# The last layer of a four-layer image network: the factors of its norms formed as pairs of matmuls, an output weight and a copy moved to VectorE, and the value projections placed later in the order

## The chip, the cores and the metric

The kernel runs on one core of one Trainium2 chip, as one program. The metric is the device time of one execution in microseconds (us); for the kernel before it is the median of three runs. Engines are named as in the profile: PE is TensorE's matmul side and PEld its weight loads, DVE is VectorE, ACT is ScalarE, POOL is GpSimd, SP is SyncE, which here only issues DMAs.

## The reference, cut to what matters

Eight images of 32 x 32 positions with 256 channels go through four layers, each `x = x + layer(groupnorm(x))`. The change lies in layer 3 alone:

```
qkv = silu(x @ w_qkv.T);  q, k, v = split(qkv)             # 8 heads of 32 channels
q = rope(rms_norm(q, w_qn));  k = rope(rms_norm(k, w_kn))  # norm over the 32 channels of a head
width, sharp = from silu(x @ w_wp.T + b_wp)                # the soft disc, per position and head
scores = q . k_win / sqrt(32)                              # 7 x 7 window around each position
scores -= (1 - sigmoid((width - rel_dist) * sharp)) * 10000
out = softmax(scores) @ v_win
out = rms_norm(out, w_on)                                  # norm over all 256 channels
y = silu((out + v) @ w_out.T)
```

The rope turns q and k by the index of the head, alike for both, so it cancels in the scores and the kernel leaves it out. Each head's norm gives one factor per position and head, and the output norm one factor per position, with a weight per channel.

## The kernel before, in words

Layer 3 (`layer3`, from line 1917 on) keeps channels on the 128 partitions: an image is two halves of 128 channels, that is four heads of 32 channels each. A **chunk** J is one image b and one half c (16 chunks, `b, c = divmod(J, 2)`). A chunk has eight **groups**; a group is a pair of 8 x 8 blocks of positions with their 14 x 14 windows (196 keys), for the four heads of the chunk. There are 128 groups, and the loop at the end of `layer3` does one per iteration n, in a software pipeline. Iteration n emits, in this order: `scores(n+3)` (L1632, 16 matmuls into four PSUM buffers), `exps(n)` (L1655, four ACT exponentials), filler units due at n, `logits(n+3)` (L1645, four DVE operations that free the four buffers), `turn(n-2, 0)` (L1673 transposes, L1678 DVE copy), `finish()`, `soft(n+5)` (L2043, four ACT tanhs), `divide(n)` (L1662 DVE reciprocal, L1663 POOL product), filler units due at n + 0.5, `turn(n-2, 1)`, `finish()`, `values(n-3)` (L1689, L1697), `masked(n+5)` (L2050, POOL).

Each engine works strictly in the order of emission (`manual_schedule`). The work of a chunk other than its groups is cut into **filler units** with a due iteration (`fill.add(at, unit)`). A unit issues its matmuls and ACT work at once and may return a function; that function (`rest`) is kept in `later` and called at the next `finish()`. The units the change touches or steps around:

- `project(J, s, h)`: four matmuls (L1982) give half h (512 positions) of q, k or v (s = 0, 1, 2) in a PSUM buffer; ACT forms a tanh of it (`half_silu`, L1967). The rest is DVE (L1992, L1994), and for q and k a square on POOL (L2002).
- `roots(J, b)`: the mean squares of q and k of chunk J, and of an image's attention output where one is due, each as rows of one PSUM buffer (L2062, L2069); then ACT takes the logarithm (L2077) and exponential (L2078) with a table load before (L2076) and one after (L2043). `fac[J]` holds the factors: rows 32(2s + h) for s and h.
- `head_scale(J, s, h)`: one product of 32 rows (L2084, two matmul instructions) spreads a factor over the 32 channels of each head into a buffer of the ring; the rest is a DVE multiplication of q or k with it (L2088).
- `tail_sq`, `tail_scale(J, b, c, h)`: the same for the output norm: square on POOL (L2112), product with `won`, whose row 8 holds the weight `w_on` (L2117), DVE multiplication (L2121), POOL addition of v (L2122).
- `in_strips(J)` lays v out in strips (POOL, L2098); `vturn(J, u)`, u = 0 to 4, transposes them (`value_unit`, L1706) and copies the PSUM buffer to v on ACT (L1711).
- `output(b, m, h)`: four matmuls (L2130), the same tanh (L1967), DVE product (L2137), POOL addition (L2139), DMA out. `discs(b, u)`: L2015 and a chain of small ACT and DVE operations.

PSUM has eight buffers of 512 columns, given out in turn (`ring`, tag "m"); whoever asks for the ninth waits until the first has been read. For a chunk due at n = 8J, the order before is: k and q projections at n-12 to n-10.5, `roots` at n-8, v projections at n-7.5 and n-7, `head_scale` k at n-6 and n-5.5 and q at n-5 and n-4.5, `in_strips` at n-6, `vturn` at n-2, -1.5, -1, -0.5 and +1.5. `tail_scale` of image b stands at 16b + 30, 30.5, 31 and 31.5; outputs at 16b + 33.5, 39, 39.5 and 41.5.

`First3.early` loads layer 3's constants while layer 2 runs; its third step, `weight`, writes the two halves of `w_on` into `won` after DVE has cleared that tile (L396, L400).

Of the kernel before, what the change touches and what calls it, by code (L numbers as in the profile page):

```python
# [12 lines left out]
ALU = mybir.AluOpType  # L13
# [19 lines left out]
def shape_constants():  # L33
    f = np.float32
    p = np.arange(P)
    k = {}

    k["k_id"] = np.stack(
        [np.eye(P), (p[:, None] // 8 == p[None] // 8) / 8.0], 1
    ).astype(f)  # L40


    same = (p[:, None] // 32 == p[None] // 32).astype(np.float64)
    k["k_hd"] = np.stack([np.eye(P) - same / 32, same / 32], 1).astype(f)
    half = (1.0 / (f(10000.0) ** np.linspace(0.0, 1.0, 16, dtype=f))).astype(f)
    angle = np.repeat(half, 2)[p % 32]
    ang = (np.arange(63, dtype=f)[None] * angle[:, None]).astype(f).astype(np.float64)
    sign = np.where(p % 2 == 0, -1.0, 1.0)[:, None]
    lam = np.log(1.0 - 2.0 ** (-2.0 - 5.0 * np.arange(HEADS) / HEADS))
    i = np.arange(SIDE)  # L50
    dist = np.abs(i[:, None] - i[None])
    s = 1.0 / np.sqrt(np.exp(lam[:, None, None] * dist).sum(-1))
    n = (s * 32.0 ** -0.5)[np.arange(8).reshape(2, 4)[:, p // 32]]
    k["k_rot"] = np.concatenate(
        [np.cos(ang), np.sin(ang) * sign, n.transpose(1, 0, 2).reshape(P, 64)], 1
    ).astype(f)
    delta = np.arange(-28, 32)
    row = np.abs(delta[None] - (p // 32)[:, None])
    col = np.abs((p % 32)[:, None] - i[None])
    m = np.exp(lam[:, None, None, None] * (row[:, :, None] + col[:, None, :])[None])  # L60
    m = m * s[:, None, None, :]
    k["k_ret"] = m.reshape(HEADS, P, 60 * 32).transpose(1, 0, 2).astype(f)


    head = (p[:, None] // 64 == p[None] // 64).astype(np.float64)
    k["k_l1"] = np.stack(
        [
            np.where(p[:, None] <= p[None], 0.0, MASK_OUT),
            p[:, None] // 4 == p[None] // 4,
            np.eye(P) - head / 64,  # L70
        ],
        1,
    ).astype(f)
    two = (p[:, None] // 64 == np.arange(2)[None]).astype(f)
    k["k_l1_sel"] = np.concatenate([two / 64, np.zeros((P, 30))], 1).astype(f)


    q, kn = np.arange(64), np.arange(NWIN)
    dr = kn[None] // 14 - (q // 8)[:, None] - 3
    dc = kn[None] % 14 - (q % 8)[:, None] - 3  # L80
    ok = (abs(dr) <= 3) & (abs(dc) <= 3)
    r = np.sqrt(dr.astype(f) ** 2 + dc.astype(f) ** 2)
    win = np.stack([np.where(ok, r, 0.0), np.where(ok, 0.0, -MASK_OUT)], 1)
    k["k_win3"] = np.tile(win, (2, 1, 1)).astype(f)
    one = np.zeros((P, 32), f)
    one[:, 8] = 1.0
    k["k_sel3"] = np.concatenate(
        [(p[:, None] // 32 == np.arange(32)[None]) / 32.0, one / 256.0], 1
    ).astype(f)
    k["k_spread"] = (p[:, None] % 32 == p[None] // 32).astype(f)  # L90
    return {n: np.ascontiguousarray(v) for n, v in k.items()}


# [12 lines left out]
def layouts(inputs):  # L106
    i = {n: np.asarray(v) for n, v in inputs.items()}
    x = i["x"]
    a = {}
    a["x"] = x.reshape(-1, C).T.reshape(2, P, -1).transpose(1, 0, 2)  # L110
    a["l0_w"] = np.stack([_wt(i["L0_conv_W" + n]) for n in "qkvo"], 1)
    a["l0_gb"] = np.stack([i["L0_conv_ln_g"], i["L0_conv_ln_b"]], 1)
    a["l1_up"] = _wt(i["L1_conv_W_up"])
    a["l1_down"] = _wt(i["L1_conv_W_down"])
    a["l1_if"] = _wt(np.concatenate([i["L1_conv_W_i"], i["L1_conv_W_f"]], 0))
    a["l1_par"] = np.concatenate(
        [i["L1_conv_conv_w"].reshape(4, P, 4).transpose(1, 0, 2)]
        + [_cols(i["L1_conv_" + n])[:, :, None] for n in ("conv_b", "skip")],
        2,
    )  # L120
    a["l1_blk"] = np.stack(
        [i["L1_conv_W" + n].reshape(4, P, 4).transpose(1, 0, 2) for n in "qkv"], 1
    )
    gb = np.stack([i["L1_conv_b_i"], i["L1_conv_b_f"]], 1)
    a["l1_gb"] = np.tile(gb, (P // 8, 1))
    nw = np.zeros((4, 32, 2, 64), np.float32)
    for q in range(2):
        nw[:, q, q] = i["L1_conv_norm_w"].reshape(4, 2, 64)[:, q]
    a["l1_nw"] = nw.reshape(P, P)
    a["l2_qkv"] = _wt(i["L2_conv_qkv_w"])  # L130
    a["l2_proj"] = _wt(i["L2_conv_proj_w"])
    qkv_b = i["L2_conv_qkv_b"]
    a["l2_par"] = np.concatenate([_cols(qkv_b), _cols(i["L2_conv_proj_b"])], 1)
    idx = near_index()
    rpb = i["L2_conv_rpb"].reshape(HEADS, -1)
    a["l2_rpb"] = np.where(idx[:, None] >= 0, rpb[:, idx].transpose(1, 0, 2), MASK_OUT).astype(
        rpb.dtype
    )
    a["l3_qkv"] = _wt(i["L3_conv_w_qkv"])
    a["l3_out"] = _wt(i["L3_conv_w_out"])  # L140
    a["l3_wp"] = _wt(i["L3_conv_w_wp"])
    a["l3_bwp"] = i["L3_conv_b_wp"]
    a["l3_qkn"] = np.concatenate(
        [np.tile(i["L3_conv_w_" + n], 4) for n in ("qn", "kn")]
    )
    a["l3_on"] = i["L3_conv_w_on"].reshape(2, P)
    a.update(shape_constants())
    return {n: np.ascontiguousarray(v) for n, v in a.items()}

# [202 lines left out]
class First3(First):  # L352
# [8 lines left out]
    def early(self):  # L361
# [25 lines left out]
        def factors():  # L387
            won, spread = self.won, self.spread
            nc.vector.tensor_scalar(self.bwp, self.bwp, 0.5, None, ALU.mult)
            nc.gpsimd.tensor_scalar(self.wo, self.wo, 0.5, None, ALU.mult)  # L390
            nc.vector.tensor_mul(won[:, 0], won[:, 0], won[:, 1])
            nc.vector.scalar_tensor_tensor(
                spread[:, 0], won[:, 0], -(32.0**-0.5) / MASK_SCALE, spread[:, 0],
                ALU.mult, ALU.mult,
            )
            nc.vector.memset(won, 0.0)  # L396

        def weight():
            for h in range(2):
                nc.sync.dma_start(  # L400
                    self.won[32 * h + 8 : 32 * h + 9], a["l3_on"].unsqueeze(0)
                )

        return [loads, factors, weight]

# [1195 lines left out]
class DiscStream(Stream):  # L1601
# [100 lines left out]
    def value_unit(self, strips, dst, u):  # L1702
        ps = self.ring("vt")
        for i in range(4):
# [3 lines left out]
                strips[:, col, 8 * r : 8 * r + 8].rearrange("p i j -> p (i j)"),  # L1708
                self.K.ident,
            )  # L1710
        self.nc.scalar.copy(  # L1711
            dst[: self.PART, 4 * u : 4 * u + 4, :],
            ps[: self.PART, :].rearrange("p (s c) -> p s c", c=P),
        )
# [202 lines left out]
def layer3(tc, K, src, dst, n_img, a, first):  # L1917
    nc = tc.nc
    pairs = disc_pairs()
    with tc.tile_pool(name="l3c", bufs=1, reuse_waits="tile") as cp, tc.tile_pool(  # L1920
# [14 lines left out]
        for i in range(3):  # L1935
            st.clear(i)
        K.ring = st.ring
        bwp, sel, spread, won = first.bwp, first.sel, first.spread, first.won
        wo, win, eps = first.wo, first.win, first.eps

        gn = first.gn
# [136 lines left out]
            nc.scalar.activation(r[:n], r[:n], AF.Exp, scale=-0.5)  # L2078
            fac[J] = r

        def head_scale(J, s, h):
            g = slice(32 * (2 * s + h), 32 * (2 * s + h) + 32)
            ps = st.ring("fac_ps")
            nc.tensor.matmul(ps, spread[g, s], fac[J][g], start=True, stop=True)  # L2084

            def rest():
                d = dest(J, s, h)
                nc.vector.tensor_mul(d, d, part(ps))  # L2088

            return rest  # L2090

# [11 lines left out]
        def vturn(J, u):  # L2103
            b, c = divmod(J, 2)
            if u == 0:
                st.v[b, c] = wk.tile([P, st.slots, P], F32, name="v", bufs=2)
            st.value_unit(strips, st.v[b, c], u)


        def tail_sq(b, c):  # L2110
            sqs["o", c] = wk.tile([P, L], F32, name="sq", bufs=4)
            nc.gpsimd.tensor_mul(sqs["o", c], st.o[b, c], st.o[b, c])  # L2112

        def tail_scale(J, b, c, h):
            g, hs = slice(32 * h, 32 * h + 32), slice(h * HALF, (h + 1) * HALF)
            ps = st.ring("fac_ps")
            nc.tensor.matmul(ps, won[g, c], fac[J][g], start=True, stop=True)  # L2117

            def rest():
                d = st.o[b, c][:, hs]  # L2120
                nc.vector.tensor_mul(d, d, ps)  # L2121
                nc.gpsimd.tensor_add(d, d, vT[b, c][:, hs])  # L2122

            return rest

# [26 lines left out]
        def plan_chunk(J):  # L2152
# [4 lines left out]
            for i in range(4):  # L2157
                s, h = 1 - i // 2, i % 2
                fill.add(n - 12 + i / 2, lambda s=s, h=h: project(J, s, h))
                fill.add(n - 6 + i / 2, lambda s=s, h=h: head_scale(J, s, h))  # L2160
            fill.add(n - 7.5, lambda: project(J, 2, 0))
            fill.add(n - 7, lambda: project(J, 2, 1))
            fill.add(n - 6, lambda: in_strips(J))

        def plan_image(b):
            n = 16 * b
# [12 lines left out]
                    fill.add(n - 10 + u / 2, lambda u=u: discs(b, u))  # L2179
            for c in range(2):  # L2180
                fill.add(n + 19 + c, lambda c=c: tail_sq(b, c))
                for h in range(2):
                    fill.add(
                        n + 30 + c + h / 2,
                        lambda c=c, h=h: tail_scale(2 * b + 4, b, c, h),
                    )
            for i in range(4):
                at = n + 32 + (1.5, 7, 7.5, 9.5)[i]
                fill.add(at - 3, lambda i=i: reload(b, i // 2, i % 2))
# [28 lines left out]
        def start():  # L2218
# [15 lines left out]
            masked(0)  # L2234
            roots(0, None)
            in_strips(0)
            for i in range(4):
                head_scale(0, 1 - i // 2, i % 2)()
            masked(1)
            for i in range(3, 9):  # L2240
                st.clear(i)
# [88 lines left out]
```

## Time and profile before

| | |
|---|---|
| runs before | 3370.86, 3371.83, 3379.88 us; median 3371.83 us |
| profiled execution | 3368.94 us, span 3367.2 us, mean granted clock 0.974 |
| PE busy | 3206.9 us, 95% of the span |
| ACT, DVE, POOL busy | 2247.9 us (67%), 2177.8 us (65%), 1490.2 us (44%) |
| DMA | 268.00 MB, mean 80 GB/s |

The page divides busy time by the whole span. In the list of windows each row gives a stretch, its length, and then for each engine the busy microseconds and the number of instructions, in the order PE, PEld, DVE, ACT, POOL, then the TensorE clock granted in that stretch (1.00 is full speed), the share of the DMA engines and GB/s. In the timeline and the chain of waits a row begins with its start and its length, then engine, line and tile; "xN" counts instructions that were merged, and square brackets give idle time before it and what ended it. In the list of groups a row gives line, engine, operation, result and operands, shape, count, then busy us and the mean ns of one, then the engine's idle time before them.

### The profile page before, as it was taken

Reading aid. Unit: us, or ns where it says so; the run is one execution under the profiler, and the core shown is the slowest. Engines: PE = TensorE matmul, PEld = TensorE weight load, DVE = VectorE, ACT = ScalarE, POOL = GpSimd, SP = SyncE. Lnnn points to the kernel's source line nnn. Section 1 sums busy time; section 2 is a strip of 40 time slices with the busy share of each in tenths; the row PEclk is TensorE's granted clock in tenths of the full one; section 3 lists DMA queues with packets and bytes.
Section 4 is the critical chain, followed back from the end, with each engine's and each line's share of the span. In section 5 each row is a group of like instructions: output and inputs, shape, how many; then the busy total and the mean of one; then the engine's idle time right before and its main releaser. Section 6 shows DMA issues by size and latency. Waiting matters only on the chain.

```text
span 3367.2 us, 77570 instructions
## 1 busy us (share of the span) xinstructions
PE 3206.9 (95%) x30760; PEld 1646.7 (49%) x30760; DVE 2177.8 (65%) x5559; ACT 2247.9 (67%) x5040; POOL 1490.2 (44%) x1069
## 2 busy tenths in 40 slices
PE   7999999999998998899999989999998999999997
PEld 3323323323222444666666755666664555555554
DVE  4776776776675666555555565666665667777775
ACT  3666666766666668554554446667776788889885
POOL 4233233223321011244444445343435667888777
PEclk9999999999999999999999999999999779999999
DMA  3000000000001666767777733111111001111001
GB/s 139 14 26 1 26 26 1 26 17 11 26 7 39 240 225 217 231 182 181 195 194 184 211 91 101 46 58 52 40 49 48 14 14 33 32 34 39 27 27 61
DMA packets 138911, 268.00 MB, mean 80 GB/s; under 512 B 9202, under 2 KB 77172, under 8 KB 130228
## 3 DMA queue, kind: packets, MB, share of 16 engines
q1 hardware_dynamic: 132164, 242.67, 23.7%
q10 hardware_dynamic: 6384, 20.37, 1.9%
q8 instruction: 243, 3.98, 0.5%
q14 instruction: 120, 0.98, 0.1%
HBM read 177.81 MB, written 85.20 MB: 78 GB/s over the span
## 4 chain that ended last, share of the span: by engine, by line
PE 71%; ACT 9%; DVE 6%; POOL 6%; issue 4%; DMA 3%; POOLq 0%; ACTq 0%; SPq 0%; DVEq 0%
PE s L675 7%; PE sm L693 6%; PE num L720 6%; PE qkv_ps L1763 5%; PE qkv_ps L1982 4%; PE dn_ps L1310 3%; PE up_ps L849 3%; PE qk_ps L550 3%; PE pt L1545 3%; PE pt L1673 2%; PE fac_ps L2084 2%; ACT e L2043 2%; PE o_ps L603 2%; PE pr_ps L1823 2%; PE o L1564 2%
## 5 line engine op out<-in xcount | busy, mean ns | idle before, releaser
L681 DVE TENSOR_TENSOR e<-s,ret 128x1024 f32<-128x1024 f32 x512 | 602.9, 1219 | 180.5 <-PE s L675 176.5
L685 ACT ACTIVATE ea<-e 128x1024 f32<-128x1024 f32 x512 | 535.1, 1054 | 268.1 <-DVE e L681 234.1
L675 PE MATMUL s<-qk,qk 32*128 32x512 f32 x2048 | 300.5, 640 | 2.4 <-POOL qk L567 1.7
L1531 POOL TENSOR_TENSOR e<-e,su 128x616 f32<-128x616 f32 (+2 forms) x128 | 157.3, 1229 | 270.3 <-DVE su L1530 239.2
L693 PE MATMUL sm<-ea,ones 128*32 128x512 f32 x2048 | 273.0, 604 | 2.0 <-DVE dn L701 2.0
L720 PE MATMUL num<-e,v 128*32 128x512 f32 x2048 | 266.6, 592 | 0.0
L1678 DVE COPY pts<-pt 112x512 f32<-112x512 f32 x256 | 175.9, 687 | 133.9 <-PE pt L1673 132.4
L2043 ACT ACTIVATE e<-win,disc 128x196 f32<-128x196 f32 x512 | 239.6, 544 | 0.2
L849 PE MATMUL up_ps<-x,wup 128*128 128x512 f32 x512 | 232.4, 606 | 4.8 <-ACT sz L889 2.3
L1663 POOL TENSOR_TENSOR e<-e,su 128x784 f32<-128x784 f32 x128 | 191.4, 1495 | 87.1 <-DVE su L1662 59.8
L1655 ACT ACTIVATE e<-e,mx 128x196 f32<-128x196 f32 x512 | 228.0, 453 | 0.0
L2050 POOL TENSOR_TENSOR e<-e,win 128x784 f32<-128x784 f32 x128 | 201.8, 1577 | 38.1 <-issue 31.5
L1526 ACT ACTIVATE e<-e,mx 128x154 f32<-128x154 f32 (+2 forms) x512 | 212.1, 425 | 0.0
L1053 POOL TENSOR_TENSOR d<-cmask,d 128x1024 f32<-128x1024 f32 x64 | 152.4, 2386 | 105.7 <-DMA d<-l1rows 105.7
L1982 PE MATMUL qkv_ps<-xq,w 128*128 128x512 f32 x384 | 192.0, 627 | 1.2 <-ACT fac L2077 1.2
L1062 ACT ACTIVATE d<-d,cols 128x128 f32<-128x128 f32 x512 | 164.0, 392 | 43.3 <-POOL d L1053 43.2
L1763 PE MATMUL qkv_ps<-x,w 128*128 128x512 f32 x384 | 181.3, 609 | 1.6 <-POOL x L236 1.6
L1673 PEld LDWEIGHTS pt<-idg,e 128*112 128x112 f32 x1024 | 120.5, 139 | 121.1 <-issue 89.9
L675 PEld LDWEIGHTS s<-qk,qk 32*128 32x128 f32 x2048 | 85.3, 183 | 184.2 <-issue 119.1
L1305 POOL TENSOR_TENSOR num<-num,sz 128x512 f32<-128x512 f32 x64 | 81.4, 1272 | 207.6 <-ACT vt L1106 109.6
L1673 PE MATMUL pt<-idg,e 128*112 128x128 f32 x1024 | 165.1, 287 | 8.4 <-DVE oT L1697 3.1
L876 DVE SCALAR_TENSOR_TENSOR cv<-xm,par,cv 128x512 f32<-128x512 f32 x192 | 140.7, 750 | 47.0 <-ACT cv L871 44.1
(243 smaller groups left out, 6711.7 us busy)
## 6 DMA issues: line engine op xcount, KB each, us to landing
d<-l1rows SPq DMA_DIRECT2D x64, 512.0 KB
x<-x SPq DMA_DIRECT2D x25, 1024.0 KB
x<-x SPq DMA_DIRECT2D x32, 512.0 KB
l1xm<-xm SPq DMA_DIRECT2D x16, 1024.0 KB
l1sz<-sz SPq DMA_DIRECT2D x16, 1024.0 KB
xv<-l1xm SPq DMA_DIRECT2D x32, 512.0 KB
l1xa<-xa SPq DMA_DIRECT2D x16, 1024.0 KB
xa<-l1xa SPq DMA_DIRECT2D x16, 1024.0 KB
```

The source lines that it names most:

```text
L675: nc.tensor.matmul(s[:, j % 2], qk[b, 1, c][g, kb * P : (kb + 1) * P], qk[b, 0, c][g, h * HALF : (h + 1) * HALF], start=True, stop=True,)
L681: nc.vector.tensor_mul(e[n, i], s, m)
L685: nc.scalar.activation(ea[n, i], e[n, i], AF.Abs)
L693: nc.tensor.matmul(acc["sm"][g, :], ones, ea[n, j // 2][:, j % 2, :], start=kb == 0, stop=kb == 7,)
L720: nc.tensor.matmul(acc["num"][g, :], v[b][:, kb, vc], e[n, j // 2][:, j % 2, :], start=kb == 0, stop=kb == 7,)
L849: nc.tensor.matmul(ps, wup[:, kc, m * P : (m + 1) * P], seg(s)[:, kc], start=kc == 0, stop=kc == 1,)
L1526: self.nc.scalar.activation(p[:, j], p[:, j], AF.Exp, scale=-1.0, bias=mx[:, j : j + 1], accum_out=su[:, j : j + 1],)
L1655: self.nc.scalar.activation(e[:, j], e[:, j], AF.Exp, scale=-1.0, bias=mx[:, j : j + 1], accum_out=self.su[:, j : j + 1],)
L1673: self.nc.tensor.transpose(ps[: self.PART, at : at + P], self.tile(n)[:, 2 * i + j, k * self.PART : (k + 1) * self.PART], self.K.ident,)
L1763: nc.tensor.matmul(ps, w[:, kc, o : o + P], x[b][:, kc, h * HALF : (h + 1) * HALF], start=kc == 0, stop=kc == 1,)
L1982: nc.tensor.matmul(ps, w[:, kc, o : o + P], xq[b][:, kc, h * HALF : (h + 1) * HALF], start=kc == 0, stop=kc == 1,)
L2043: nc.scalar.activation(e[:, j], win[:, 0], AF.Tanh, scale=disc[b][:, i, 8 + h : 9 + h], bias=disc[b][:, i, h : h + 1],)
```

## The change

`head_scale` now forms both halves h of one s: two products, one after the other, into two buffers, and then two DVE multiplications in its rest. `tail_scale` takes one half h of both channel halves c: the factor is spread once, by a matrix of ones (`k_one8`), into one buffer, and the weight `w_on` comes in as a per-partition operand of a DVE `scalar_tensor_tensor`, once for each c. `vturn` returns its copy as a rest, and the copy is a DVE `tensor_copy`. The v projections move from n-7.5 and n-7 to n-5.5 and n-4.5, `in_strips` from n-6 to n-4, and the `head_scale` pairs stand at n-6 (k) and n-5 (q). `tail_scale` stands at 16b + 30 and 31. The constant tile is filled by one DMA of 64 KB and one of 128 rows of two numbers, without clearing.

```diff
 def weight():
-    for h in range(2):
-        nc.sync.dma_start(
-            self.won[32 * h + 8 : 32 * h + 9], a["l3_on"].unsqueeze(0)
-        )
+    nc.sync.dma_start(self.won[:, 0], a["k_one8"])
+    nc.sync.dma_start(self.won[:, 1, 0:2], a["l3_on"])
...
 def value_unit(self, strips, dst, u):
...
-        self.nc.scalar.copy(
+        return lambda: self.nc.vector.tensor_copy(
             dst[: self.PART, 4 * u : 4 * u + 4, :],
             ps[: self.PART, :].rearrange("p (s c) -> p s c", c=P),
         )
...
-        def head_scale(J, s, h):
-            g = slice(32 * (2 * s + h), 32 * (2 * s + h) + 32)
-            ps = st.ring("fac_ps")
-            nc.tensor.matmul(ps, spread[g, s], fac[J][g], start=True, stop=True)
+        def head_scale(J, s):
+            ps = [st.ring("fac_ps") for _ in range(2)]
+            for h in range(2):
+                g = slice(32 * (2 * s + h), 32 * (2 * s + h) + 32)
+                nc.tensor.matmul(ps[h], spread[g, s], fac[J][g], start=True, stop=True)
             def rest():
-                d = dest(J, s, h)
-                nc.vector.tensor_mul(d, d, part(ps))
+                for h in range(2):
+                    d = dest(J, s, h)
+                    nc.vector.tensor_mul(d, d, part(ps[h]))
...
-            st.value_unit(strips, st.v[b, c], u)
+            return st.value_unit(strips, st.v[b, c], u)
...
-        def tail_scale(J, b, c, h):
+        def tail_scale(J, b, h):
             g, hs = slice(32 * h, 32 * h + 32), slice(h * HALF, (h + 1) * HALF)
             ps = st.ring("fac_ps")
-            nc.tensor.matmul(ps, won[g, c], fac[J][g], start=True, stop=True)
+            nc.tensor.matmul(ps, ones[g], fac[J][g], start=True, stop=True)
             def rest():
-                d = st.o[b, c][:, hs]
-                nc.vector.tensor_mul(d, d, ps)
-                nc.gpsimd.tensor_add(d, d, vT[b, c][:, hs])
+                for c in range(2):
+                    d = st.o[b, c][:, hs]
+                    nc.vector.scalar_tensor_tensor(
+                        d, d, on[:, c : c + 1], ps, ALU.mult, ALU.mult
+                    )
+                    nc.gpsimd.tensor_add(d, d, vT[b, c][:, hs])
...
                 fill.add(n - 12 + i / 2, lambda s=s, h=h: project(J, s, h))
-                fill.add(n - 6 + i / 2, lambda s=s, h=h: head_scale(J, s, h))
-            fill.add(n - 7.5, lambda: project(J, 2, 0))
-            fill.add(n - 7, lambda: project(J, 2, 1))
-            fill.add(n - 6, lambda: in_strips(J))
+            for s in range(2):
+                fill.add(n - 5 - s, lambda s=s: head_scale(J, s))
+            fill.add(n - 5.5, lambda: project(J, 2, 0))
+            fill.add(n - 4.5, lambda: project(J, 2, 1))
+            fill.add(n - 4, lambda: in_strips(J))
...
-                for h in range(2):
-                    fill.add(
-                        n + 30 + c + h / 2,
-                        lambda c=c, h=h: tail_scale(2 * b + 4, b, c, h),
-                    )
+                fill.add(n + 30 + c, lambda c=c: tail_scale(2 * b + 4, b, c))
```

The start of layer 3 calls `head_scale` for chunk 0 in the same order as before (k, then q), now as two pairs. Layers 0 to 2 are the same but for the two loads.

More of the change, by code (lines that the diff above doesn't have):

```diff
@@ L90, in shape_constants @@
     k["k_spread"] = (p[:, None] % 32 == p[None] // 32).astype(f)
+    k["k_one8"] = np.tile(p[:, None] % 32 == 8, (1, P)).astype(f)
     return {n: np.ascontiguousarray(v) for n, v in k.items()}
@@ L145, in layouts @@
     )
-    a["l3_on"] = i["L3_conv_w_on"].reshape(2, P)
+    a["l3_on"] = _cols(i["L3_conv_w_on"])
     a.update(shape_constants())
@@ L395, in factors @@
             )
-            nc.vector.memset(won, 0.0)
         def weight():
-            for h in range(2):
-                nc.sync.dma_start(
-                    self.won[32 * h + 8 : 32 * h + 9], a["l3_on"].unsqueeze(0)
-                )
+            nc.sync.dma_start(self.won[:, 0], a["k_one8"])
+            nc.sync.dma_start(self.won[:, 1, 0:2], a["l3_on"])
         return [loads, factors, weight]
@@ L1937, in layer3 @@
         K.ring = st.ring
-        bwp, sel, spread, won = first.bwp, first.sel, first.spread, first.won
+        bwp, sel, spread = first.bwp, first.sel, first.spread
+        ones, on = first.won[:, 0], first.won[:, 1, 0:2]
         wo, win, eps = first.wo, first.win, first.eps
@@ L2236, in start @@
             in_strips(0)
-            for i in range(4):
-                head_scale(0, 1 - i // 2, i % 2)()
+            for s in (1, 0):
+                head_scale(0, s)()
             masked(1)
```

## The prediction

> **What bounds the kernel now.** I began with the busy times: PE has 95% of the span, and only layer 3 (from about 2565 us on) is touched, so the whole span's averages were put aside. The list of windows, cut at the places where an undisturbed image changes its kind of work (it takes 91.2 us), shows what each stretch is limited by.
>
> ```profile
> 3011.80:3037.60 25.80, 24.60 (x271) 16.00 (x264) 18.38 (x71) 20.64 (x65) 21.11 (x16) 1.00 0.14 45
> 3037.60:3059.90 22.30, 22.24 (x234) 11.18 (x234) 17.75 (x71) 21.79 (x64) 15.32 (x13) 1.00 0.23 70
> 3059.90:3081.70 21.80, 21.80 (x242) 12.25 (x234) 17.07 (x65) 17.30 (x51) 20.60 (x17) 1.00 0.01 2
> 3081.70:3103.00 21.30, 20.05 (x233) 10.19 (x225) 16.16 (x64) 21.22 (x56) 17.05 (x13) 1.00 0.09 27
> ```
>
> PE (first number after the length) is full in the third and nearly so in all. But where the roots are (rows two and four), ACT (fourth number) is full as well: 21.79 of 22.30, 21.22 of 21.30. So PE sets the pace with ACT a fraction behind. The chain of waits shows how, behind one `roots`:
>
> ```profile
> 2899.47 0.63 ACT fac L2078
> 2900.11 1.28 ACT L2043
> ...
> 2907.77 0.48 ACT th L1967
> 2908.25 0.48 ACT v L1711
> 2908.73 0.04 issue
> 2908.78 1.12 PE fac_ps L2084 x2
> 2909.90 0.58 PE pt L1673 x4
> 2910.48 1.05 PE fac_ps L2084 x2
> ```
>
> The factor products wait for ACT's queue, and each costs PE 1.05 to 1.12 us. The timeline of PE has the same products once standing together, in the start of the layer:
>
> ```profile
> 2579.72 1.14 PE L2084 MATMUL fac_ps<-fac,spread 32*128 32x512 f32 x8 [1.97 <-ACT fac L2078]
> 2580.79 5.40 PE L1982 MATMUL qkv_ps<-xq,w 128*128 128x512 f32 x8
> ```
>
> Eight instructions, four products of 32 rows each, take as long as one does alone. Last, windows of 10 us over the first images:
>
> ```profile
> 2650.00:2660.00 10.00, 6.57 (x64) 3.59 (x62) 3.88 (x11) 9.92 (x26) 4.20 (x3) 0.99 0.01 2
> 2660.00:2670.00 10.00, 9.83 (x92) 4.92 (x92) 8.30 (x33) 10.00 (x33) 7.46 (x6) 0.50 0.01 2
> 2670.00:2680.00 10.00, 10.00 (x72) 4.59 (x57) 5.85 (x28) 1.26 (x6) 3.27 (x3) 0.50 0.00 0
> ```
>
> Behind the roots PE stood still for 3.4 us, and in the 20 us that follow it got half its clock; there a factor product takes 2.00 us.
>
> **The parts, and PE's own account.** Pairs: 15 chunks (chunk 0's four already stand together) times two pairs, each 1.1 us in place of 2 x 1.05: 31.5 us less PE. Output norm: 16 products in place of 32, 16 x 1.05 = 16.8 us less; its DVE and POOL operations stay 32 each (677 ns at L2121; the same shape with another operand, L2137, has 683). Turned values: 80 copies of 573 ns (L1711, 45.8 us) leave ACT, and DVE gets 80 of the shape of L1678, 687 ns, spaced by 0.60 us when queued. PE would be 48 us shorter, about 54 with the products at half clock. That would be the gain if PE stayed the only bound. So I go stretch by stretch for what is late next.
>
> **Roots to the k projection (rows two and four).** The two v projections (1.85 us each) leave the gap behind the roots. Let M be the end of the mean-square matmuls. PE's work up to the first factor product is then pt 0.58, pt 0.44, o 0.58, s 0.52, pt 0.58, out 1.96, vt 0.44, pt 0.44, o 0.58, s 0.66: M + 6.8. In the changed order the second product of the pair takes the PSUM buffer that the output's product held eight before. That one is freed by DVE's L2137, which waits for ACT's tanh, which stands behind L2077 0.70, L2078 0.63, table 1.28, soft 1.78, exps 1.77 and soft 1.78: M + 7.95; tanh 0.6 and DVE 0.65 make M + 9.2. On DVE the v copy, the oT copies and the next logits are queued behind L2137, and PE's next transposes wait for that v copy (0.6 more, within the product's 1.1). So PE idles about 1.4 to 2.4 us, then goes on: product 1.07, pt 0.58, v 1.75, pt 0.44, o 0.58, s 0.52, q pair 1.1, pt 0.58, v 1.75, pt 0.44, o 0.58, s 0.52, with 0.2 of waiting for DVE: the k projection starts at M + 19.3. Before it took 19.5 (row two, 22.3 less 2.8 for the matmuls of the roots) and 20.2 (row four's kind, 2897.4 to 2917.6). Of 2.1 us saved on PE per chunk, 0.2 and 0.85 remain: the projections now cost PE time where they had been filling a wait.
>
> **The other two stretches.** Row one ends in a chain through ACT (tanhs, exps, v copies); three v copies of 0.47 to 0.56 go from it, and one DVE operation of 0.68 comes into it: -0.8. In row three two output products go, -2.1 on PE, but DVE now has per iteration logits 1.13, pts 1.2, recip 0.1, oT 0.3, two L2121 1.2 and two v copies 1.2 = 5.1 us, plus 0.6 waiting for its first transposes, against PE's 4.5: the roots come only 0.7 earlier.
>
> **What is at nothing.** `in_strips` moves two iterations later past POOL's other work; its readers, the transposes at n-2, come some 11 us after it, POOL being busy 21.1 of 25.8 us in row one; if that cover failed, 1.8 us per chunk, 27 in all. The two loads of `weight` are issued by SP at 2422.7 (254 ns each now; a 128 KB load took 327 ns to issue), 370 us before the first use; the 1 MB image load behind them on SP could start later by the transfer, which for 256 KB took 2.79 us at the end of the chain. The clearing on DVE (272 ns) goes.
>
> **The sum.** From chunk 5 on: 5 x 0.2 + 6 x 0.85 + 6 x 0.8 + 6 x 0.7 = 15.1 us. Chunks 1 to 4 have no output product behind their roots, so nothing holds the pair's buffer: the time from M to the k projection was 22.6, 26.0, 25.7 and 24.0, mean 24.6, with half clock for most of it. By the same account it is 17.5 at full clock and about 26 if half clock stays for all of it; the pause there shrinks from 2.6 to 3.4 us to about 2.1 (PE's own work ends at M + 4.9, and it waits for exps, 6.2, and a DVE copy, 7.0). I take 20.5, nearer to the middle since the trace shows no pause of that length in just this place: 4 x 4 = 16. The two short drops of the clock near 2870 and 2965 (24.0 in place of 22.3 in the second) may go with the fuller array: 1.7. The end, ACT's copies and the earlier first output: 2. Together 35 us: 3368.9 of the profiled execution becomes 3334; the median stands 2.9 above that execution, so 3337.
>
> [...]
>
> **Rivals.** *Slower, by the clock.* The place is the gap behind the roots, no longer filled by 3.7 us of dense projections; the mechanism is the one seen at 2650: a pause, then half clock. That stretch took 6.5 us more than the undisturbed one; with pairs I price a drop at 5. In all eleven later chunks it is 55 us against 35 gained: about 3392. It decides from seven such chunks on. For it: 0.50 followed each of the first pauses. Against: pauses of 1.1 us at 2904 left the clock at 1.00, and pairs with projections between them fill more of the array than lone products. *PE stays the bound,* if ACT, freed of 5.7 us per image, runs further ahead than my order allows: 54 us, about 3318. For it: no other engine is above 81 us in 91. Against: the buffer held by the tanh. *No gain:* v copies on DVE stand behind operations that wait for ACT, hold PSUM buffers and so PE; or the pairs do not overlap inside the loop, which the row at 2579 speaks against. Either takes back some 30 us: about 3367.
>
> **How the numbers follow.** Forecast 0.51, PE-bound 0.19, no gain 0.15, slower by the clock 0.15. About 0.3% (10 us) is what a measurement of this kernel can tell from no change. Faster by more: 0.93 of the forecast, all of PE-bound, 0.15 of no gain: 0.69. Within: 0.04 + 0.12, 0.16. Slower: 0.15. The range goes from beyond PE-bound, 3312, to 3374, which takes in no gain and the forecast with half clock kept in the first chunks (3353); it leaves out the clock rival.
>
> **What would show it.** Right: `fac_ps` shows four instructions in 1.1 us; images take 88 to 89 us in place of 91.2; PE idles before the second product, ended by DVE L2137 or the copies; ACT's copies are gone. Wrong: images of 86 us or less (PE-bound), granted clock 0.5 around each roots (slower), or PE waiting longer for DVE's v copies than the copies took on ACT (no gain).

## The result, and the profile after

| | before | after |
|---|---|---|
| median of 8 runs each | 3371.59 us (3370.17 to 3379.88) | 3385.09 us (3382.06 to 3389.05) |
| ratio, 95% interval | | 1.0036 (1.0025 to 1.0047) |
| profiled execution, span | 3368.94, 3367.2 us | 3386.9, 3385.1 us |
| PE, DVE, ACT busy | 3206.9, 2177.8, 2247.9 us | 3184.4, 2223.7, 2212.3 us |

The changed kernel is slower by 0.36%, some 12 us, where 35 us less were forecast. PE has 22.5 us less to do than before and still ends later. Line numbers have shifted: `head_scale` is now L2086 (product) and L2091, the tail L2121 (product) and L2126, the copy of turned values L1710, the tanh's product of the output L2144, the input norm still L418.

The loss is not everywhere. From the first `wp_ps` matmuls of one image (the products of `discs`, L2015) to those of the next it took 74.6, 104.2, 95.2, 92.7, 94.3, 91.2 and 91.2 us before, and 161.9 from the eighth image's to the end. After, it takes 70.6, 89.7, 94.8, 99.8, 98.1, 99.8, 98.1 and 171.0. The first three stretches gained 18.9 us, the rest lost 35.5. The list of windows for a later image, cut at the same kinds of work as the four rows ahead of the prediction (columns: stretch, length, busy us and instructions of PE, PEld, DVE, ACT, POOL, granted clock, DMA share, GB/s), shows where:

```profile
3007.10:3031.10 24.00, 22.68 (x256) 15.02 (x256) 19.81 (x73) 18.59 (x60) 18.60 (x16) 1.00 0.08 30
3031.10:3056.60 25.50, 23.61 (x243) 11.91 (x235) 19.78 (x73) 19.39 (x56) 14.69 (x11) 0.87 0.20 64
3056.60:3077.90 21.30, 20.64 (x235) 12.06 (x230) 18.09 (x68) 18.58 (x58) 21.24 (x18) 1.00 0.01 2
3077.90:3107.00 29.10, 23.96 (x236) 12.12 (x233) 17.91 (x69) 19.97 (x53) 19.56 (x14) 0.88 0.12 34
```

Rows one and three are shorter, by 1.8 and 0.5 us. The two stretches behind the roots are longer, by 3.2 and 7.8 us, and in them alone the clock is below 1.00. PE's timeline behind the second of these roots (its mean-square matmuls end at 3079.01):

```profile
3084.81 0.59 PE L1631 MATMUL s<-kp,qT 32*64 32x196 f32 x16
3086.32 1.09 PE L2086 MATMUL fac_ps<-fac,spread 32*128 32x512 f32 x2 [0.92 <-DVE pts L1677]
3088.41 2.07 PE L2086 MATMUL fac_ps<-fac,spread 32*128 32x512 f32 x2 [1.00 <-DVE th L2144]
3090.41 1.10 PE L1672 MATMUL pt<-idg,e 128*112 128x128 f32 x4
3091.30 3.41 PE L1982 MATMUL qkv_ps<-xq,w 128*128 128x512 f32 x4
```

The pair is torn apart by its buffer, as forecast; but the second product then takes 2.07 us in place of 1.07, the transposes 1.10 in place of 0.60, the moved v projection 3.41 in place of 1.88. Two stretches over the same place, cut where the granted clock (the third number from the end) changes:

```profile
3084.14:3087.55 3.41, 2.35 (x44) 1.01 (x42) 0.95 (x3) 3.41 (x12) 2.83 (x2) 1.00 0.00 0
3087.55:3094.38 6.83, 5.97 (x10) 2.62 (x11) 4.86 (x18) 3.62 (x13) 3.52 (x3) 0.50 0.25 78
```

Half clock begins early in the second pause, 2.2 us after the last scores ended (3085.40), and lasts 6.83 us. Against full speed, 1.0 + 0.5 + 1.5 makes 3.0 us at this place. Row four loses more than that, and ACT's timeline, then PE's a little later, say why:

```profile
3094.75 0.60 ACT L1967 ACTIVATE th<-qkv_ps 128x512 f32<-128x512 f32 x1 [3.59 <-PE qkv_ps L1982]
3099.65 1.24 ACT L418 ACTIVATE xq<-x,gn 128x1024 f32<-128x1024 f32 x1 [4.30 <-PE qkv_ps L1982]
```

```profile
3103.84 1.12 PE L1982 MATMUL qkv_ps<-xq,w 128*128 128x512 f32 x2 [1.64 <-ACT xq L418]
3106.97 1.52 PE L1982 MATMUL qkv_ps<-xq,w 128*128 128x512 f32 x3 [1.56 <-DVE vT L1994]
```

ACT stands still for 4.3 us ahead of the input norm of the *next* image (L418). That norm writes `xq`, which the projections read, into one of three shared buffers, whose last reader is the second v projection of the previous image's odd chunk: the very matmuls that the change moved from n-7 to n-4.5, that is past the norm's own due time (16b - 13.5 against 16b - 12.5). With ACT in order, the exponentials and the tanhs behind the norm wait too, then PE. Over five images (the window from 2720 to 3220 us) the list of waits has (engine, line, what it waited for; us, times, longest):

```profile
ACT xq L418 <- PE qkv_ps L1982: 23.0, 5, 4.8
PEld qkv_ps L1982 <- ACT xq L418: 13.8, 10, 2.5
PE qkv_ps L1982 <- ACT xq L418: 8.2, 5, 1.6
```

In the trace of before no such wait stood out.

### The profile page after: what moved, and what is told of

It reads as the page before. It is cut to its first block, busy times and chain, and to the rows that moved or that the text cites. A ratio compares the mean times of both kernels' runs of the same rounds, so it can differ in the third digit from the quotient of the medians.

```text
span 3385.1 us, 77573 instructions
## 1 busy us (share of the span) xinstructions
PE 3184.4 (94%) x30728; PEld 1644.2 (49%) x30728; DVE 2223.7 (66%) x5638; ACT 2212.3 (65%) x4960; POOL 1490.4 (44%) x1069
## 4 chain that ended last, share of the span: by engine, by line
PE 71%; ACT 8%; DVE 8%; POOL 5%; issue 4%; DMA 3%; SPq 0%; POOLq 0%; ACTq 0%; DVEq 0%
PE s L674 7%; PE sm L692 6%; PE num L719 6%; PE qkv_ps L1762 5%; PE qkv_ps L1982 5%; PE dn_ps L1309 3%; PE up_ps L848 3%; PE pt L1544 3%; PE qk_ps L549 3%; PE pt L1672 2%; PE o_ps L602 2%; PE pr_ps L1822 2%; PE o L1563 2%; PE num_ps L1209 2%; ACT e L2043 2%
## 5 line engine op out<-in xcount | busy, mean ns | idle before, releaser
L1982 PE MATMUL qkv_ps<-xq,w 128*128 128x512 f32 x384 | 209.0, 672 | 25.1 <-ACT xq L418 11.4
```

The source lines that it names most:

```text
L1982: nc.tensor.matmul(ps, w[:, kc, o : o + P], xq[b][:, kc, h * HALF : (h + 1) * HALF], start=kc == 0, stop=kc == 1,)
```

## The experiments

Two theories were set against each other: **A**, the move of the v projections costs more than the rest gains, by the clock behind each roots and by the norm's wait; **B**, VectorE's additional work (copies, L2126) costs it. Each run was timed beside runs of the kernel before on the same chip; ratios with their 95% intervals are what is compared across chips, and 0.001 is 3.4 us.

**The move alone, and all but the move.** To the kernel before:

```diff
-            fill.add(n - 7.5, lambda: project(J, 2, 0))
-            fill.add(n - 7, lambda: project(J, 2, 1))
-            fill.add(n - 6, lambda: in_strips(J))
+            fill.add(n - 5.5, lambda: project(J, 2, 0))
+            fill.add(n - 4.5, lambda: project(J, 2, 1))
+            fill.add(n - 4, lambda: in_strips(J))
```

> The kernel before, with only the values' projections and the strips moved to 5.5, 4.5 and 4 steps ahead of the chunk; factor products, tail and the engine of the turned values as before. Theory A (the move is what costs: it opens a gap on PE behind every roots in which the clock falls to half, +3.3 us per roots, and the input norm of the next image waits on ACT for the moved projection, +5.3 us per image): slower than before, about 3400 to 3420 us, with a clock row of 0.50 behind each roots and ACT's xq waiting several us for PE. Theory B (the extra work on VectorE is what costs): 3372 us, give or take 5, and full clock behind the later roots.

Measured: 3436.01 us, ratio 1.0178 (1.0150 to 1.0206); images from 97.8 us (the second) to 105.8 (the fifth to seventh). PE behind one roots:

```profile
3119.91 1.09 PE L2084 MATMUL fac_ps<-fac,spread 32*128 32x512 f32 x2 [2.09 <-DVE pts L1678]
3121.83 1.07 PE L1673 MATMUL pt<-idg,e 128*112 128x128 f32 x4 [0.83 <-ACT v L1711]
3122.83 2.07 PE L2084 MATMUL fac_ps<-fac,spread 32*128 32x512 f32 x2
```

Again the times of half clock, behind two pauses round a lone product: the transposes take 1.07 us where the next, at 3128.13, take 0.60, and the product 2.07 where the next takes 1.12. ACT's `xq` waits 22.2 us, in four waits, within the same window of 500 us. Without pairs and with the copies on ACT the move costs 60 us, more than theory A had priced; no VectorE work is needed for it.

The reverse edit to the changed kernel (the three lines back):

> The changed kernel with the values' projections and the strips back in their old places (7.5, 7 and 6 steps ahead); pairs, output norm and copies as changed. Theory A (the move costs): about 3342 us, images of about 87.5 us, full clock behind the later roots, no long wait of ACT's xq. Theory B (the extra work on VectorE costs): 3375 us or more, no better than the changed kernel by over 10 us.

Measured: 3332.14 us, ratio 0.9870 (0.9844 to 0.9895); images of 88.5 to 90.7 us from the third on. All else of the change together is worth 44 us; B falls. One of its images:

```profile
2989.80:3079.60 89.80, 86.18 (x961) 50.45 (x953) 75.56 (x277) 76.06 (x223) 74.06 (x56) 0.98 0.12 37
```

**What in the move costs: the norm's wait.** First the norm was put later, in the changed kernel:

```diff
-                    fill.add(n - 13.5 + c / 2, lambda c=c: normed(b, c))
+                    fill.add(n - 12.4 + c / 4, lambda c=c: normed(b, c))
```

> The changed kernel with the input norm of the next image due at 12.4 and 12.15 steps ahead of it in place of 13.5 and 13, so that ACT meets it behind the exponentials and behind the tanh of the projection whose buffer it reuses; all else as changed. If the wait of the norm (about 5 us per image, seven images) is a cost of its own: about 3355 us, images of 93 to 94 us. If all of the loss is the clock: 3385 us. If the norm is then late for the projection of the queries that follows it: between 3370 and 3385, with PE waiting for xq there.

Measured: 3379.51 us, ratio 1.0011 (0.9994 to 1.0028): the third case, a gain of a few us (0.0025). ACT's wait is gone from the list, but the projections that read `xq` still meet it late, by a little more than the 13.8 and 8.2 us of the changed kernel:

```profile
PEld qkv_ps L1982 <- ACT xq L418: 16.2, 10, 2.4
PE qkv_ps L1982 <- ACT xq L418: 10.2, 5, 2.0
```

PE's share of the wait had stayed, so this run could not price it. A second way leaves the norm where it is and releases its buffer sooner:

```diff
-            fill.add(n - 4.5, lambda: project(J, 2, 1))
+            fill.add(n - (5.5 if J % 2 else 4.5), lambda: project(J, 2, 1))
```

> The changed kernel, with the second values' projection of odd chunks directly behind the first (both 5.5 steps ahead), so that the input norm's buffer is released about one step (some 5 us) earlier while the gap behind the roots stays; even chunks as changed. If the norm's wait costs about 5 us per image by itself: most of it goes, images of 94 to 96 us, 3355 to 3365 us, half clock still behind every roots. If the loss of the odd chunks' move is all clock: 3380 us or more.

Measured: 3366.01 us, ratio 0.9976 (0.9967 to 0.9986), 0.0060 or 20 us below the changed kernel. No wait of as much as 1 us for or by `xq` is left in the list, while an image still has a reduced clock:

```profile
2912.70:3008.40 95.70, 89.38 (x960) 50.68 (x952) 76.13 (x278) 76.47 (x224) 73.98 (x56) 0.95 0.11 35
```

These 20 us need not all be the wait's: the edit also puts two dense projections next to each other, and the fourth to seventh images have 0.95, 0.95, 0.98 and 0.96 here against 0.93, 0.95, 0.93 and 0.95 in the changed kernel. Together they are 16.7 us shorter, and up to 9 of these can be clock (each length times the share of the clock that is missing).

**What in the move costs: the clock.** In the changed kernel, ahead of the values of the group that stands in the gap, two dense products (`dense` is the output's weight) whose result is overwritten by the real ones:

```diff
...
+        if n % 8 == 6 and self.dense is not None:
+            for _ in range(2):
+                self.nc.tensor.matmul(
+                    o, self.K.ident, self.dense, start=True, stop=True,
+                    skip_group_check=True,
+                )
```

> The changed kernel with two dense matmuls of 128x128 by 512 added behind every roots, ahead of the first values, into the buffer of the values that the real ones then overwrite: they keep PE busy where it paused. If the clock falls because of that pause: full clock behind the later roots and about 3350 us (3.3 us less for each of 11 roots, less what of the two products does not fit into the pause). If the clock falls for something else: 3385 to 3409 us (14 times up to 1.7 us more) and 0.50 still behind the roots.

Measured: 3368.88 us, ratio 0.9972 (0.9956 to 0.9988): 22 us less, although PE has more to do. Behind an even chunk's roots:

```profile
3034.53 1.88 PE L1687 MATMUL o<-wo,idg 128*128 128x512 f32 x4
3037.44 1.12 PE L2094 MATMUL fac_ps<-fac,spread 32*128 32x512 f32 x2
3038.78 1.12 PE L2094 MATMUL fac_ps<-fac,spread 32*128 32x512 f32 x2 [0.21 <-DVE th L2152]
3039.83 0.65 PE L1673 MATMUL pt<-idg,e 128*112 128x128 f32 x4
3040.31 1.88 PE L1990 MATMUL qkv_ps<-xq,w 128*128 128x512 f32 x4
```

Products, transposes and projection are at full speed here. Behind the odd chunk's roots 43 us later the same sequence still fell to half: its v projection took 3.11 us, and the 10 us from 3080 have 0.83. So the fill removed about one drop of two, and the expectation of 3.3 us for each of 11 was too much for it: 16 us by the medians, 22 by the ratios. Three stretches of 3.41 us, the first from the even gap, the others from the odd one (cut where the clock changes there, and a whole number of such steps ahead):

```profile
3037.64:3041.05 3.41, 3.19 (x10) 1.26 (x10) 2.98 (x11) 3.41 (x13) 2.25 (x2) 1.00 0.03 12
3078.60:3082.01 3.41, 3.17 (x45) 1.27 (x44) 1.92 (x6) 3.41 (x13) 2.21 (x2) 1.00 0.00 0
3082.01:3085.42 3.41, 3.41 (x8) 1.91 (x8) 3.14 (x14) 1.78 (x5) 1.93 (x3) 0.50 0.25 82
```

PE is as busy in the second as in the first, 3.17 and 3.19 us, yet only the second is followed by half clock. The first ends with 0.7 us of the v projection; the second holds values, scores and two lone products, for the dense products ended at 3078.63, just as it began. That work was added and time went down, while the fourth to seventh images have a granted clock of 0.98 against 0.93 to 0.95 in the changed kernel, shows that it is the clock, and not PE's work, which costs there.

Both edits in one kernel:

> The same, with two dense matmuls of 128x128 by 512 added behind every roots as in the filled kernel. If waits of the norm and clock add: the filled kernel gained 16 us, so 3340 to 3350 us, images of 91 to 93. If they are one and the same loss: no better than the better of the two, 3360 us or more.

Measured: 3343.96 us, ratio 0.9916 (0.9901 to 0.9931), 0.0120 below the changed kernel. The single gains are 0.0060 and 0.0064: they add, so the two edits take away two different losses. An image of it:

```profile
2992.30:3084.00 91.70, 88.73 (x969) 50.59 (x961) 75.98 (x278) 76.56 (x224) 74.09 (x56) 1.00 0.11 36
```

0.0046 (0.0006 to 0.0087 by the ends of both intervals), some 15 us, remains to the kernel without the move. Part of it lies in the last image, whose stretch takes 171.0 us here and 162.6 there. The dense products themselves, 16 times 1.88 us, are a likely part too: PE is busy 88.73 us in the image above and 86.18 in the one without the move. The rest of it was not traced.

**Which chunks.** The odd chunks' v projections and strips back, the even ones as changed:

```diff
-            fill.add(n - 5.5, lambda: project(J, 2, 0))
-            fill.add(n - 4.5, lambda: project(J, 2, 1))
-            fill.add(n - 4, lambda: in_strips(J))
+            d = 2 if J % 2 else 0
+            fill.add(n - 5.5 - d, lambda: project(J, 2, 0))
+            fill.add(n - 4.5 - d * 1.25, lambda: project(J, 2, 1))
+            fill.add(n - 4 - d, lambda: in_strips(J))
```

> The changed kernel with the values' projections of odd chunks (and their strips) back in the old places, 7.5, 7 and 6 steps ahead; those of even chunks stay at 5.5, 4.5 and 4. The input norm's buffer is read last by an odd chunk's projection. If the norm's wait (about 5 us per image) and the clock behind each roots (about 3.3 us each, two per image) are both costs of the move: images of 93 to 94 us, about 3350 us, half clock left behind the even chunks' roots alone, ACT's xq without a long wait. If only the clock counts: about 3362. If only the even chunks' move is at fault: 3380 or more.

Measured: 3337.73 us, ratio 0.9890 (0.9873 to 0.9908); images of 89.6 to 92.5 us from the third on. Nearly all of the loss, 0.0146 of 0.0166, is the odd chunks' move, better than the 3350 expected. What is left sits behind the even chunks' roots: within the image

```profile
3000.00:3010.00 10.00, 8.51 (x112) 4.67 (x108) 6.96 (x27) 8.91 (x22) 6.72 (x5) 1.00 0.27 80
3010.00:3020.00 10.00, 9.64 (x64) 4.48 (x63) 7.79 (x30) 6.21 (x23) 5.84 (x4) 0.66 0.18 55
```

and in no other row from 2982.7 to 3070 is the clock below 1.00. With the dense products behind the even chunks' roots alone (`n % 16 == 6`):

> The same as the kernel with the odd chunks' projections back, with two dense matmuls of 128x128 by 512 added behind the even chunks' roots, into the buffer of the values that the real ones overwrite. If both causes are the whole of the loss: as fast as the changed kernel without the move within about 6 us (3332 to 3340), images of 90 to 91 us. If something else of the move costs time as well: 3345 or more.

Measured: 3330.76 us, ratio 0.9869 (0.9850 to 0.9888), the same as without the move. So with the gap filled nothing measurable is left of the even chunks' move. The odd chunks' move is undone in this kernel; with both remedies and both moves the 15 us above remained.

**What the other parts bring.** Pairs alone, in the kernel before (projections in their old places; `head_scale` as in the change):

```diff
...
-                fill.add(n - 6 + i / 2, lambda s=s, h=h: head_scale(J, s, h))
+            for s in range(2):
+                fill.add(n - 5 - s, lambda s=s: head_scale(J, s))
```

> The kernel before with the factor products in pairs (both ahead of their two multiplications, one step later for each half), and nothing else changed. By the prediction's account for PE, 15 chunks with two pairs at 1.05 us each: 31.5 us less, about 3341 us. If ACT, nearly full behind the roots, takes over there: 3355 to 3372 us, with PE idle behind the roots.

Measured: 3335.60 us, ratio 0.9882 (0.9862 to 0.9903): 40 us, as much as pairs, tail and copies have together. Its images take 68.4, 86.7, 88.6, 89.0, 89.0, 91.1 and 91.0 us: 30 us come from the first three, 9 from the next two, and the last two, which ran at full clock (1.00) before, gain nothing, although PE has 2.0 us less to do in each (88.6 to 86.6 in the seventh). Where the kernel before had 0.50 in both of the rows from 2660 to 2680 shown ahead of the prediction, this has:

```profile
2660.00:2670.00 10.00, 9.66 (x109) 5.72 (x108) 9.59 (x40) 10.00 (x33) 7.19 (x6) 0.84 0.01 2
2670.00:2680.00 10.00, 10.00 (x106) 5.45 (x105) 8.46 (x36) 5.72 (x20) 7.36 (x7) 0.89 0.01 2
```

The pause ahead of it is as long as before (2.77 us, `DVE vT L1994`), but only some 5.4 of these 20 us are at half clock (twice 1.6 and 1.1 us), where before all were. Behind the second roots of this image it does not fall at all: the 30 us from 2690 have 1.00 throughout, where before the 30 us from 2700 had 0.88, 0.50 and 0.50. The first three stretches had a granted clock of 0.82, 0.79 and 0.91 before and have 0.88, 0.96 and 0.98 now: by length times missing share 44 us were lost there, now 13.5. The difference, 30 us, is as much as they got shorter; by this account what pairs gain in the first images is clock.

The copies and the tail were then separated. The changed kernel without the move, with the copies on ACT at the deferred place (the copy is still a `rest`, called at the next `finish()`):

```diff
-        return lambda: self.nc.vector.tensor_copy(
+        return lambda: self.nc.scalar.copy(
```

> The changed kernel with the projections in their old places, and with the copies of turned values on ACT again (80 copies of about 573 ns). If the copies on VectorE relieve ACT where it sets the pace behind the roots: 5 to 15 us slower than without the move alone, 3337 to 3347 us. If they only make PE wait for VectorE (1.2 us once per image, 0.5 us more at the scores): 5 to 10 us faster, 3322 to 3327 us.

Measured: 3345.89 us, ratio 0.9917 (0.9897 to 0.9937). The same at their old place (`self.nc.scalar.copy(` issued at once), which is pairs and tail:

> Pairs and the changed output norm, with the copies of turned values on ACT at their old place in the order; projections as before. By the prediction's account the tail's 16 products less are 16.8 us of PE: 3319 to 3330 us. If VectorE takes over there (740 ns in place of 677 for each of 32 operations, two in a row): 3336 us or more, no gain over pairs alone, with the scores waiting for VectorE's L2126.

Measured: 3340.61 us, ratio 0.9904 (0.9889 to 0.9920). And pairs with the copies on VectorE, the tail as before:

> Pairs alone, and with them the copies of turned values on VectorE as in the change; output norm and projections as before. Pairs alone gave 3336 us; pairs with the tail and the copies on VectorE 3332, and that with the copies back on ACT (where the deferred place in the order was kept) 3346. If the copies on VectorE gain about 10 us and the output norm's change loses about as much: 3320 to 3328 us. If the place of the copy, and not its engine, made the 14 us of difference: about 3336.

Measured: 3329.92 us, ratio 0.9873 (0.9860 to 0.9886). The tail adds nothing: 0.9904 against 0.9882 with copies on ACT, 0.9870 against 0.9873 with copies on VectorE, the intervals overlapping both times. The copies' engine is worth 0.0009 without the tail and 0.0034 with it, overlapping again, and 0.0047 at the deferred place, where the intervals do not meet; this last is more than the other two, so part of it can be the place. The lists of waits of the five images say what happened to the tail's saved products. First pairs alone, then pairs and tail:

```profile
PE out_ps L2133 <- ACT e L1655: 5.5, 5, 1.1
```

```profile
PE out_ps L2137 <- ACT e L1654: 12.2, 5, 2.5
```

With ACT still copying, 6.7 us of what PE saves on the tail in five images (some 10.5) becomes waiting for ACT's exponentials. With the copies on VectorE that row is gone, and pairs with copies have in its place

```profile
PE pt L1673 <- DVE v L1711: 6.0, 5, 1.2
```

and with the tail also 3.2 us of scores waiting for L2126, which in the changed kernel takes 741 ns where I had put in the 677 of its predecessor:

```profile
L2126 DVE SCALAR_TENSOR_TENSOR oT<-oT,won,fac_ps 128x512 f32<-128x512 f32 x32 | 22.3, 741 | 0.0
```

Pairs with copies, 3329.9 us, and the whole change with only even chunks moved and filled, 3330.8, are the fastest versions found, and the changed kernel without the move, 3332.1, is not told apart from them by its interval; all beat before by some 40 us and after by over 50.

## Why the prediction was wrong

*What bounds the kernel* was read rightly: PE sets the pace with ACT a fraction behind, and a later run shows ACT taking over where only PE is relieved further (pairs with tail).

*PE's own account* was near in its total, partly by luck. The 128 factor matmuls cost 82.3 us before and 46.7 with pairs alone, 35.6 less, for 31.5. But 14 of the 60 lone products before took 2.1 us at half clock, and of the 30 pairs only ten took 1.1 us, 18 took 1.6 to 1.7. After, they cost 60.5: 12 of the 30 pairs were torn apart, and eight of these 24 lone products ran at half clock. The tail's products went from 33.4 to 16.8, as put down, and no gain from them could be measured, because other engines were late next. That was the prediction's own rule: it gave rows one and three only 0.8 and 0.7 us an image for the tail and the copies, which is too little to be told apart here.

*Roots to the k projection*, the order of the queues: the second product of the pair was put at M + 9.2, and came at M + 9.4 (M = 3079.01, 3088.41); the pause of 1.4 to 2.4 us was 1.92 (0.92 + 1.00), its releasers DVE's product behind the tanh and a DVE copy. **This step failed in what follows**, which goes on at full clock through "product 1.07, pt 0.58, v 1.75". The pause was counted for its own length alone. The rows have these at 2.07, 1.10 and 3.41 us, and the k projection began at M + 22.1 (3101.08) in place of M + 19.3. The paragraph on the rivals had seen half clock follow the first pauses and kept it at 0.15, on the strength of pauses of 1.1 us that had left 1.00. The rival's place and mechanism were right: it named the gap that dense projections no longer fill. Its price was 5 us a drop; about 3 us is what the rows show, and 22 us in all is what a partial fill won back. That its total, 3392, came close to the 3385 measured is in part luck, for it leaves out the wait that comes next.

**The step that was missing** is the one for an added wait. I listed who reads what `in_strips` writes, and the queues that it passes, but not what the moved *matmuls* read: the release of `xq`'s buffer moved with them past the writer of the next image. Written as due times it is one line, n-4.5 = 16b - 12.5 against 16b - 13.5. Releasing the buffer in time won 20 us, some of it perhaps clock, and no rival contained this wait.

*The first chunks* were put at 16 us, and the first three stretches gained 18.9 even so; without the move they gain 37, with pairs alone 30. One reading under this term was off: 22.6, 26.0, 25.7 and 24.0 us are counted from ACT's logarithm (L2077); from M, the end of the mean-square matmuls, PE's timeline of before has 24.8, 29.6, 29.3 and 24.2 to the k projection. The 1.7 us for two short drops of the clock rested on an estimate that a fuller array ends them. With pairs alone the fourth and fifth stretches have 1.00 where before had 0.98 and 0.96, and are 9 us shorter together; that the fuller array did it was not shown. *The whole* would have held without the move: 35 us forecast, 44 measured. That agreement is partly luck, for the gain came from the pairs and the clock, and not in the shares of the sum: 16 for the early chunks was too small, 15.1 for the later ones too large by what the images at full clock show.

How the clock went, as the traces show it: 0.50 began early in the second of two pauses of 0.92 and 1.00 us, 2.2 us from the last scores on, and the 3.4 us for which PE stood still in the row at 2650 are two pauses, 0.61 and 2.77 us. In layer 3 of the kernels before and after, every stretch at 0.50 begins a whole number of steps of 3.413 us after the one before (in the changed kernel 3043.18, 3087.55 and 3142.17, 44.37 and 54.62 us apart, so 13 and 16 steps) and lasts a whole number of them, one or two in the changed kernel and one to seven before, but for the last, at the end of the program. What decides between 1.00 and 0.50 was not shown: the rows of the filled kernel have two steps of like busy time, 3.19 and 3.17 us, with unlike outcome. The rival of no gain had VectorE's copies hold up PE; measured, the copies on VectorE were no slower in any of three comparisons, and faster beyond the intervals in one.

## What to carry to other kernels

When work is moved later, list what it reads as well as what it writes: a buffer is released by its last reader, and the next writer may stand in another engine's queue ahead of the new place. When dense work is taken out of a gap, price the gap by the clock that follows it, not by its length, and do not count on a small product inside it: here pauses of 0.92 and 1.00 us with a product of 1.09 between them went with 6.83 us at 0.50. And test the parts of a bundle apart: here one part held all of the gain that could be measured, and one edit of three lines gave back more.

## What the runs showed of the hardware that was not expected

Half clock did not need a long standstill: 0.50 set in at the second of two pauses of 0.92 and 1.00 us (and behind two of 2.09 and 0.83 in the move alone) with only a 32-row product of 1.09 us between. In the changed kernel it lasted 6.83 us; in the move alone it shows in transposes of 1.07 us in place of 0.60 and a product of 2.07 in place of 1.12. In the filled kernel it followed a step of 3.41 us in which PE was busy for 3.17 us, with values, scores and two lone products but next to nothing of the dense ones. In the traces of before and after its stretches in layer 3 begin whole steps of 3.413 us apart (13 steps from 3043.18 to 3087.55), and of two gaps filled alike one kept its clock (1.00) and one lost it (0.50).

The other side of this: after the same pause of 2.77 us, the clock stayed at 0.50 for 20 us with lone factor products, while with products in pairs the same two rows had 0.84 and 0.89. Adding two dense products of 1.88 us together behind every roots made the kernel 22 us faster.
